# Four graph layers on one core: row ends of the last layer with one product of 128 columns, and GpSimd for their SBUF-only steps

## The chip, the cores and the metric

The kernel runs on one core of one Trainium2 chip. A core has five engines, each with its own queue that is worked off in order: TensorE (PE) multiplies matrices and writes to PSUM, VectorE (DVE) and ScalarE (ACT) compute element by element and read SBUF and PSUM, GpSimd (POOL) computes element by element on SBUF, and SyncE (SP) issues DMAs. The engines wait for each other through semaphores. The time is that of one execution on the device, in microseconds; the metric is the median over several runs.

## The reference

Four layers follow each other over 4096 nodes with 64 features and one weighted adjacency matrix `adj` (4096 x 4096, fp32, all entries at or above zero); each layer's result is added to its input and normalized over the features. Only the last layer, a hyperbolic aggregation, is touched:

```python
c = CURV
deg = jnp.maximum(adj.sum(axis=1, keepdims=True), 1e-08)
w = adj / deg
log_ij = _logmap(x[:, None, :], x[None, :, :], c)
agg = jnp.einsum('ij,ijc->ic', w, log_ij)
transformed = agg @ weight + bias
origin = jnp.zeros_like(transformed)
return _expmap(origin, transformed, c)
...
x = _layernorm(x + _L3_gnn_ref(x, adj, L3_gnn_weight, L3_gnn_bias), axis=-1)
```

`_logmap` of a pair (i, j) is a factor of the pair times a combination of x_i and x_j, so that the sum over j needs, for each row i, a weighted sum of the x_j and a scalar that multiplies x_i. The exponential map at the origin scales each row by tanh of its norm over its norm.

## The kernel before

All of this is the last stage of one program, "layer 3", from line 1423 on. The 4096 nodes are cut into eight groups of 512 (`GB` = 4 blocks of 128). `seq` gives the order of the groups: 4, 5, 6, 7, 0, 1, 2, 3. As the factor of a pair is the same for (i, j) and (j, i), only tiles (i, j) with j at or after i in `seq` are computed, 36 tiles of 512 x 512. Each is done in two halves, so that the loop `while n < NU + 2 ...` runs over 72 units.

In a unit PE multiplies the features (`product`, `opposite`, lines 1493 and 1512), ACT takes five passes over 128x1024 values (square, logarithm, exponentials: lines 1502, 1691, 1692, 1718, 1727), and DVE three products or comparisons of that size (1701, 1704, 1716), a cheap one (1520), and two products of 128x512 with the transposed factors (1540, or 1533 on the diagonal). `gather` then sums on PE: line 1554 the tile's own rows, lines 1562 and 1566 the mirrored ones. The sums go to `tb`, [128, 4096]: its lower half holds a group's own row sum, its upper half the mirrored one (copies on ACT, lines 1573 and 1576). `at_d` and `at_m` are the tiles of `adj`, loaded by SP up to three tiles ahead.

When the last tile of a group's row is summed, `finals(g)` makes the six steps of the group's row end, and they are put on a list, `seam`; every unit takes one step from it. The steps are: nothing; `first`, the products of `tb` with `spread` (the two halves added, 65 columns) and the scalar `al` of each row; `second`, products with `spread_w` (the same with the layer's weight) and of the row's own x with `wh_x`, and from them `v`; `third`, the squared norm of `v` on ACT and its square roots by logarithm and exponential; `fourth`, tanh over norm, applied to `v`, and x added; `fifth`, the layernorm and the output DMA. Six of the eight groups have their row end inside the loop; those of groups 2 and 3, the last in `seq`, are left over when it ends and are done by the last lines, which take a step of one and a step of the other in turn.

The order of the instructions on each engine's queue is set by the tile framework, which places the steps' instructions between those of the units by its own estimate of when they are ready; DVE, ACT and PE work each queue strictly in that order. Tiles come from rotating pools: `r3` holds two buffers of each name (`al`, `v`, `vn`), `ps_p3` two PSUM banks, `post`.

Of the kernel before, what the change touches and what calls it, by code (L numbers as in the profile page):

```python
# [9 lines left out]
F32 = mybir.dt.float32  # L10
# [52 lines left out]
def gnn4_kernel(  # L63
# [22 lines left out]
    P = 128  # L86
# [178 lines left out]
    def layernorm(dst, y, by_ln=False, by_scale=False):  # L265
# [26 lines left out]
        nc.vector.tensor_tensor(dst, y, over_rows(mv[:, :, 0]), ALU.subtract)  # L292
        nc.vector.tensor_tensor(dst, dst, over_rows(r), ALU.mult)
# [1132 lines left out]
    with tc.tile_pool(name="o3", bufs=1) as op, tc.tile_pool(name="cols3", bufs=3) as cols_p, tc.tile_pool(  # L1426
# [9 lines left out]
        spread_w = op.tile([P, F], F32, name="spread_w")  # L1436
# [106 lines left out]
        def gather(t, h, tm):  # L1543
# [30 lines left out]
            if t is not None and h and tiles[t][1] == seq[-1]:  # L1574
                g = tiles[t][0]
                work.append(lambda: nc.scalar.copy(tb[0:F, gcols(g)], bank[0:F, :]))
                seam.extend(finals(g))
            return work

        def factors(ps_p):  # L1580
# [7 lines left out]
            nc.vector.tensor_copy(kappa[:, 1, :], t)  # L1588
# [3 lines left out]
        def weights(ps_p):  # L1592
# [5 lines left out]
            nc.tensor.matmul(ps[:, 0:F], lhsT=t, rhs=wh, start=True, stop=True)  # L1598
            nc.vector.tensor_copy(spread_w, ps[:, 0:F])
# [3 lines left out]


        def finals(g):
# [5 lines left out]
            vn = rp.tile([P, GB, 2], F32, name="vn")  # L1611

            def first(ps_p):
                ps = ps_p.tile([P, GB, F + 1], F32, name="post", tag="post")
                for b in range(GB):
                    nc.tensor.matmul(ps[:, b, :], lhsT=tb[:, cols(g * GB + b)], rhs=spread, start=True, stop=True)
                sq = sm.tile([P, GB, F], F32, name="sq3", tag="t0")
                nc.vector.tensor_tensor(sq, xg, ps[:, :, 0:F], ALU.mult)
                nc.vector.tensor_reduce(al, sq, AX.X, ALU.add)
                nc.vector.scalar_tensor_tensor(al, al, 2.0, ps[:, :, F], ALU.mult, ALU.subtract)  # L1620
                nc.vector.tensor_tensor(al, al, kappa[:, 1, gs], ALU.mult)

            def second(ps_p):
                o = ps_p.tile([P, GB, 2, F], F32, name="post", tag="post")
                for b in range(GB):
                    jb = g * GB + b
                    nc.tensor.matmul(o[:, b, 0, :], lhsT=tb[:, cols(jb)], rhs=spread_w, start=True, stop=True)
                    nc.tensor.matmul(o[:, b, 1, :], lhsT=tr_c[:, jb // 2, :], rhs=wh_x[:, jb % 2, :], start=True, stop=True)
                t = sm.tile([P, GB, F], F32, name="agg", tag="t0")
                for b in range(GB):  # L1630
                    jb = g * GB + b
                    nc.scalar.activation(v[:, b, :], o[:, b, 0, :], AF.Copy, scale=kappa[:, 0, jb : jb + 1])
                nc.vector.tensor_tensor(t, o[:, :, 1, :], over_rows(al), ALU.mult)
                nc.vector.tensor_tensor(t, t, bh.unsqueeze(1).to_broadcast([P, GB, F]), ALU.add)
                nc.vector.tensor_tensor(v, v, t, ALU.add)

            def third(ps_p):

                sq = sm.tile([P, GB, F], F32, name="sqv", tag="t0")
                n = sm.tile([P, GB], F32, name="nv")  # L1640
                for b in range(GB):
                    nc.scalar.activation(sq[:, b, :], v[:, b, :], AF.Square, accum_out=n[:, b : b + 1])
# [5 lines left out]
            def fourth(ps_p):  # L1648
# [7 lines left out]
                nc.vector.tensor_tensor(v, v, over_rows(th), ALU.mult)  # L1656
                nc.vector.tensor_tensor(v, v, xg, ALU.add)

            def fifth(ps_p):
                o_sb = sm.tile([P, GB, F], F32, name="o_sb")  # L1660
                layernorm(o_sb, v, by_ln=True, by_scale=True)
# [17 lines left out]
        while n < NU + 2 or turns or gathers:  # L1679
# [45 lines left out]
            if 0 < n <= NU:  # L1725
                rt = rts[n - 1][:, :, columns(n - 1)]
                nc.scalar.activation(rt, rt, AF.Ln, scale=1.0 / SCALE)  # L1727
            if seam:
                seam.pop(0)(ps_p)
# [55 lines left out]
```

## Time and profile before

| | |
|---|---|
| median of 3 runs | 1419.52 us (1418.89 to 1420.07) |
| profiled execution | 1422.83 us, of which the span is 1421.0 us |
| busy over the span | PE 1322.2 us, DVE 1049.9, ACT 805.8, POOL 99.1 |
| instructions of POOL | 175 |
| granted TensorE clock, mean | 0.972 |
| first steps of the eight row ends (line 1618) begin at | 1091.8, 1169.9, 1236.2, 1294.8, 1339.7, 1374.0, 1395.3, 1397.1 us |
| last products into the sums end at | 1392.4 us |
| last output step ends at | 1417.7 us |

A line of the timeline gives start and duration in us, the engine, the line of the kernel, the operation, the tile written and those read, and their sizes (partitions x elements); in brackets, the idle time of the engine before it and what ended it. A line of the waits gives who waited for whom, the total in us, how often, and the longest. A line of the chain gives start, length and the engine, tile and line that the end of the program hung on at that time. A group's line gives its count, its total and mean time, and the idle time before it. Instructions overlap a little on one engine, so that the time that one takes from its engine is read from its start to the start of the next.

### The profile page before, as it was taken

To read this page: it belongs to the slowest core of one execution; us is meant where nothing else is said; L and a number is where in the kernel's file an instruction comes from. 1 tells how busy PE (TensorE), PEld (TensorE's weight loads), DVE (VectorE), ACT (ScalarE), POOL (GpSimd) and SP (SyncE) were. 2 spreads that over 40 slices of the span, in tenths; PEclk is the share of its full clock that TensorE was granted. 3 is DMA by queue.
4 is the path that set the end of the run, shared out by engine and by line. 5 is a ranking of instruction groups with operands and counts; after the bars stand their busy time and mean duration, and the time that the engine had idled before them with its cause. 6 is when DMAs were issued, how large, how long until landed. Compare 5 with 4: busy or idle time off the path is not lost.

```text
span 1421.0 us, 19096 instructions
## 1 busy us (share of the span) xinstructions
PE 1322.2 (93%) x6830; PEld 616.2 (43%) x6830; DVE 1049.9 (74%) x2016; ACT 805.8 (57%) x1346; POOL 99.1 (7%) x175
## 2 busy tenths in 40 slices
PE   7999999999999998999999999997988898989894
PEld 5655555555344333444443323333333333434433
DVE  7699999998343266878884224357999999998995
ACT  4654444343000116654422675745989999999993
POOL 2111111110132000000110000000000000000000
PEclk9999999999999999999998999998999999999996
DMA  9999999999699999999985555534245344544410
GB/s 321 403 394 415 409 415 415 411 404 393 217 365 389 382 421 378 372 348 335 328 308 178 177 177 175 174 124 178 107 161 207 147 183 152 217 150 170 181 64 11
DMA packets 108191, 382.16 MB, mean 269 GB/s; under 512 B 20276, under 2 KB 20280, under 8 KB 76472
## 3 DMA queue, kind: packets, MB, share of 16 engines
q1 hardware_dynamic: 87096, 296.17, 56.3%
q0 software_dynamic: 12736, 76.29, 13.0%
q10 hardware_dynamic: 8256, 8.39, 1.7%
q8 instruction: 56, 0.92, 0.2%
q14 instruction: 47, 0.39, 0.1%
HBM read 294.05 MB, written 85.20 MB: 267 GB/s over the span
## 4 chain that ended last, share of the span: by engine, by line
PE 64%; ACT 16%; DVE 12%; DMA 5%; issue 2%; ACTq 0%; SPq 0%; DVEq 0%
PE a_ps L1111 8%; PE pass L566 7%; PE tp L657 7%; PE w_ps L566 5%; PE p_ps L1102 5%; PE pass L559 5%; PE cnt_ps L1373 4%; DMA raw<-in_adj_dram 4%; PE h_ps L559 4%; PE acc_ps L1333 4%; ACT w L1691 2%; ACT w L1502 2%; DVE at_m L1540 2%; ACT rt L1692 2%; ACT rt L1727 2%
## 5 line engine op out<-in xcount | busy, mean ns | idle before, releaser
L664 ACT COPY at<-tp 128x512 f32<-128x512 f32 x248 | 127.8, 598 | 118.2 <-issue 95.0
L1378 ACT ACTIVATE wt<-cnt_ps 128x512 uint16<-128x512 f32 x208 | 115.5, 595 | 73.1 <-PE cnt_ps L1373 68.2
L688 DVE TENSOR_REDUCE dpart<-raw 128x4 f32<-128x2048 f32 x64 | 145.5, 2274 | 4.0 <-DMA raw<-in_adj_dram 3.9
L1554 PE MATMUL sums_ps<-at_d,some 128*64 128x512 f32 x288 | 146.2, 628 | 2.0 <-DVE at_d L1533 1.8
L690 DVE TENSOR_REDUCE lows<-raw 128x1 f32<-128x2048 f32 x64 | 145.5, 2273 | 0.0
L657 PE MATMUL tp<-ident,raw 128*128 128x128 f32 x1024 | 130.8, 281 | 7.9 <-DMA raw<-in_adj_dram 6.6
L657 PEld LDWEIGHTS tp<-ident,raw 128*128 128x128 f32 x1024 | 114.5, 143 | 45.4 <-issue 35.1
L1111 PE MATMUL a_ps<-at,nat_a 128*64 128x512 f32 x512 | 123.4, 610 | 0.0
L1566 PE MATMUL sums_ps<-at_m,some 128*64 128x512 f32 x224 | 110.5, 616 | 0.0
L1493 PE MATMUL v_ps<-rv,tr_a 64*128 64x512 f32 (+1 forms) x288 | 81.9, 647 | 21.8 <-DVE rt L1716 21.6
L566 PE MATMUL pass<-at,cheb_n 128*128 128x512 f32 x224 | 99.2, 601 | 2.4 <-DVE cheb_n L588 1.9
L566 PE MATMUL w_ps<-at,cheb_n 128*128 128x512 f32 x208 | 93.5, 593 | 0.0
L1716 DVE SCALAR_TENSOR_TENSOR rt<-v_ps,rt 128x1024 f32<-128x1024 f32 x72 | 83.2, 1156 | 4.3 <-ACT rt L1692 4.0
L1373 PE MATMUL cnt_ps<-m,follow 128*64 128x512 fp8e4 x480 | 81.7, 391 | 4.6 <-ACT wt L1378 2.0
L1701 DVE SCALAR_TENSOR_TENSOR f<-rt,w 128x1024 f32<-128x1024 f32 x72 | 82.8, 1156 | 2.8 <-ACT rt L1727 2.7
L1704 DVE TENSOR_TENSOR at_d<-at_d,f 128x1024 f32<-128x1024 f32 x72 | 83.0, 1153 | 0.1
L1380 DVE TENSOR_SCALAR wt<-cnt_ps 128x512 uint16<-128x512 f32 x48 | 33.2, 692 | 63.2 <-PE cnt_ps L1373 60.1
L1540 DVE TENSOR_TENSOR at_m<-post,at_m 128x512 f32<-128x512 f32 x112 | 74.6, 679 | 4.6 <-PE post L1538 4.5
L1727 ACT ACTIVATE rt<-rt 128x1024 f32<-128x1024 f32 x72 | 72.4, 1006 | 9.7 <-DVE rt L1716 9.4
L1538 PE MATMUL post<-ident,f 128*128 128x128 f32 x448 | 69.3, 284 | 7.2 <-DVE at_m L1540 6.2
L1691 ACT ACTIVATE w<-w 128x1024 f32<-128x1024 f32 x72 | 72.0, 1001 | 5.0 <-DVE w L1520 5.0
L1718 ACT ACTIVATE w<-w 128x1024 f32<-128x1024 f32 x72 | 72.3, 1006 | 0.7
(392 smaller groups left out, 2250.8 us busy)
## 6 DMA issues: line engine op xcount, KB each, us to landing
at<-adj_t SPq DMA_DIRECT2D x119, 1024.0 KB, 7.6
raw<-in_adj_dram SPq DMA_DIRECT2D x64, 1024.0 KB, 13.1
adj_t<-at POOLq DMA_DIRECT2D x62, 1024.0 KB, 8.0
at_d<-adj_t SPq DMA_DIRECT2D x36, 1024.0 KB, 4.6
at_m<-adj_t SPq DMA_DIRECT2D x28, 1024.0 KB, 6.7
m<-mask_t SPq DMA_DIRECT2D x120, 128.0 KB, 2.8
m<-mask_t SPq DMA_DIRECT2D x60, 256.0 KB, 4.2
mask_t<-mask ACTq DMA_DIRECT2D x28, 256.0 KB, 7.6
```

The source lines that it names most:

```text
L559: in_order(nc.tensor.matmul(ps[q * F : (q + 1) * F, :], lhsT=cheb_n[:, jb, k, :], rhs=rhs, start=first, stop=last, skip_group_check=True,))
L566: in_order(nc.tensor.matmul(ps, lhsT=cheb_n[:, jb, k : k + 2, :], rhs=rhs, start=first, stop=last))
L657: in_order(nc.tensor.transpose(tp[:, cols(b)], raw[:, b, cols(k)], ident))
L664: nc.scalar.copy(at[:, k, :], tp)
L688: in_order(nc.vector.tensor_reduce(dpart[:, g, c, :], raw, AX.X, ALU.add))
L690: in_order(nc.vector.tensor_reduce(lows[:, n : n + 1], raw.rearrange("p b j -> p (b j)"), AX.X, ALU.min))
L1111: in_order(nc.tensor.matmul(ps[q * F : (q + 1) * F, :], lhsT=nat_a[:, c * CB + k, 0:F], rhs=of[q if signed else 0][:, k, :], start=(c == 0 ...
L1373: in_order(nc.tensor.matmul(cnt[a][r * HP : (r + 1) * HP, :], lhsT=follow, rhs=chunks[c][odd][2 * a + r][:, k, :], start=(h == 2 * NB - 1) ...
L1378: in_order(nc.scalar.activation(wt[odd][a], cnt[a], AF.Relu, scale=-128.0))
L1540: work.append(lambda to=to, tp=tp: nc.vector.tensor_tensor(to, tp, to, ALU.mult))
L1554: in_order(nc.tensor.matmul(bank[0:F, :], lhsT=nat_c[:, j * CB + k, :], rhs=own[t][:, k, :], start=(i == j and k == 0), stop=(j == seq[-1] ...
L1566: in_order(nc.tensor.matmul(bank[F:P, :], lhsT=nat_c[:, above * GB + k, :], rhs=mirrored[tm][:, k, :], start=(k == 0 and above == seq[0]), ...
```

## The change

The change has five parts, all in the row ends of layer 3 and the step that prepares them.

- `spread` and `spread_w` stand side by side in one tile, `two_w`, and `first` makes one product of 128 columns of each block of `tb` instead of one of 65 and, later, one of 64. The extra column that `first` used is replaced by a tile `z`: x less its last feature, with -0.5 in the last column, made by GpSimd in `less_last`; kappa's second part holds twice its value.
- For the last two groups the products of x with `wh_x` are made before, by two steps (`ahead_of_last`) that are put on the list six units before the end; ACT copies them to SBUF (`turned_x`).
- For these two groups `v` is scaled by DVE in `first`, and the rest stays on DVE and ACT.
- For the other six groups GpSimd adds the bias, adds the two parts of `v`, squares `v`, and later scales `v` and adds x; DVE sums the squares, where ACT squared and summed before; and the layernorm ends with two products on GpSimd in place of four scaled outputs on ACT.
- The last copy of `tb`'s lower half goes from ACT to DVE.

In the changed kernel as built, the queue of SP keeps its order. The two steps made ahead take two places of the list, so that the steps of group 1 come two units later; its statistics and layernorm are then done after the loop.

```diff
-    def layernorm(dst, y, by_ln=False, by_scale=False):
+    def layernorm(dst, y, by_ln=False, by_scale=False, last=None):
+        last = last or nc.vector
...
-        nc.vector.tensor_tensor(dst, y, over_rows(mv[:, :, 0]), ALU.subtract)
-        nc.vector.tensor_tensor(dst, dst, over_rows(r), ALU.mult)
+        last.tensor_tensor(dst, y, over_rows(mv[:, :, 0]), ALU.subtract)
+        last.tensor_tensor(dst, dst, over_rows(r), ALU.mult)
...
-        spread_w = op.tile([P, F], F32, name="spread_w")
+        two_w = op.tile([P, 2 * F], F32, name="two_w")
+        spread_w = two_w[:, F : 2 * F]
...
-                work.append(lambda: nc.scalar.copy(tb[0:F, gcols(g)], bank[0:F, :]))
+                copy = nc.vector.tensor_copy if g == seq[-1] else nc.scalar.copy
+                work.append(lambda: copy(tb[0:F, gcols(g)], bank[0:F, :]))
...
-            nc.vector.tensor_copy(kappa[:, 1, :], t)
+            nc.vector.tensor_scalar_mul(kappa[:, 1, :], t, 2.0)
...
+            nc.vector.tensor_copy(two_w[:, 0:F], pair)
...
+        turned_x, zs = {}, {}
+
+        def less_last(g):
+            z, xg = rp.tile([P, GB, F], F32, name="z"), nat_a[:, gblocks(g), 0:F]
+            nc.gpsimd.tensor_tensor(z[:, :, 0 : F - 1], xg[:, :, 0 : F - 1], over_rows(xg[:, :, F - 1], F - 1), ALU.subtract)
+            nc.gpsimd.memset(z[:, :, F - 1], -0.5)
+            return z
+
+        def weighed_x(ps_p, g):
+            o = ps_p.tile([P, GB, F], F32, name="post", tag="post")
+            for b in range(GB):
+                jb = g * GB + b
+                nc.tensor.matmul(o[:, b, :], lhsT=tr_c[:, jb // 2, :], rhs=wh_x[:, jb % 2, :], start=True, stop=True)
+            return o
+
+        def ahead_of_last(g):
+            def step(ps_p):
+                turned_x[g] = rp.tile([P, GB, F], F32, name="xw")
+                nc.scalar.copy(turned_x[g], weighed_x(ps_p, g))
+                zs[g] = less_last(g)
+
+            return step
...
+            late = g in seq[-2:]
+            own_engine = nc.vector if late else nc.gpsimd
+
+            z = zs[g] if late else less_last(g)
...
-                ps = ps_p.tile([P, GB, F + 1], F32, name="post", tag="post")
+                ps = ps_p.tile([P, GB, 2 * F], F32, name="post", tag="post")
                 for b in range(GB):
-                    nc.tensor.matmul(ps[:, b, :], lhsT=tb[:, cols(g * GB + b)], rhs=spread, start=True, stop=True)
+                    nc.tensor.matmul(ps[:, b, :], lhsT=tb[:, cols(g * GB + b)], rhs=two_w, start=True, stop=True)
                 sq = sm.tile([P, GB, F], F32, name="sq3", tag="t0")
-                nc.vector.tensor_tensor(sq, xg, ps[:, :, 0:F], ALU.mult)
+                nc.vector.tensor_tensor(sq, z, ps[:, :, 0:F], ALU.mult)
                 nc.vector.tensor_reduce(al, sq, AX.X, ALU.add)
-                nc.vector.scalar_tensor_tensor(al, al, 2.0, ps[:, :, F], ALU.mult, ALU.subtract)
                 nc.vector.tensor_tensor(al, al, kappa[:, 1, gs], ALU.mult)
-
-            def second(ps_p):
-                o = ps_p.tile([P, GB, 2, F], F32, name="post", tag="post")
+                if late:
+                    nc.vector.tensor_tensor(v, ps[:, :, F : 2 * F], over_rows(kappa[:, 0, gs]), ALU.mult)
+                    return
                 for b in range(GB):
                     jb = g * GB + b
-                    nc.tensor.matmul(o[:, b, 0, :], lhsT=tb[:, cols(jb)], rhs=spread_w, start=True, stop=True)
-                    nc.tensor.matmul(o[:, b, 1, :], lhsT=tr_c[:, jb // 2, :], rhs=wh_x[:, jb % 2, :], start=True, stop=True)
+                    nc.scalar.activation(v[:, b, :], ps[:, b, F : 2 * F], AF.Copy, scale=kappa[:, 0, jb : jb + 1])
+
+            def second(ps_p):
                 t = sm.tile([P, GB, F], F32, name="agg", tag="t0")
-                for b in range(GB):
-                    jb = g * GB + b
-                    nc.scalar.activation(v[:, b, :], o[:, b, 0, :], AF.Copy, scale=kappa[:, 0, jb : jb + 1])
-                nc.vector.tensor_tensor(t, o[:, :, 1, :], over_rows(al), ALU.mult)
-                nc.vector.tensor_tensor(t, t, bh.unsqueeze(1).to_broadcast([P, GB, F]), ALU.add)
-                nc.vector.tensor_tensor(v, v, t, ALU.add)
+                nc.vector.tensor_tensor(t, turned_x[g] if late else weighed_x(ps_p, g), over_rows(al), ALU.mult)
+                own_engine.tensor_tensor(t, t, bh.unsqueeze(1).to_broadcast([P, GB, F]), ALU.add)
+                own_engine.tensor_tensor(v, v, t, ALU.add)
+                if not late:
+                    nc.gpsimd.tensor_tensor(z, v, v, ALU.mult)
 
             def third(ps_p):
...
+                if late:
+                    for b in range(GB):
+                        nc.scalar.activation(sq[:, b, :], v[:, b, :], AF.Square, accum_out=n[:, b : b + 1])
+                else:
+                    nc.vector.tensor_reduce(n, z, AX.X, ALU.add)
...
-                nc.vector.tensor_tensor(v, v, over_rows(th), ALU.mult)
-                nc.vector.tensor_tensor(v, v, xg, ALU.add)
+                own_engine.tensor_tensor(v, v, over_rows(th), ALU.mult)
+                own_engine.tensor_tensor(v, v, xg, ALU.add)
...
-                layernorm(o_sb, v, by_ln=True, by_scale=True)
+                layernorm(o_sb, v, by_ln=True, by_scale=late, last=own_engine)
...
+            if n == NU - 6:
+                seam += [ahead_of_last(g) for g in seq[-2:]]
```

More of the change, by code (lines that the diff above doesn't have):

```diff
@@ L1611, in finals @@
             vn = rp.tile([P, GB, 2], F32, name="vn")
+            n = rp.tile([P, GB], F32, name="nv")
+            late = g in seq[-2:]
+            own_engine = nc.vector if late else nc.gpsimd
+            z = zs[g] if late else less_last(g)
             def first(ps_p):
-                ps = ps_p.tile([P, GB, F + 1], F32, name="post", tag="post")
+                ps = ps_p.tile([P, GB, 2 * F], F32, name="post", tag="post")
                 for b in range(GB):
-                    nc.tensor.matmul(ps[:, b, :], lhsT=tb[:, cols(g * GB + b)], rhs=spread, start=True, stop=True)
+                    nc.tensor.matmul(ps[:, b, :], lhsT=tb[:, cols(g * GB + b)], rhs=two_w, start=True, stop=True)
@@ L1637, in third @@
+                if not late:
+                    nc.gpsimd.tensor_tensor(z, v, v, ALU.mult)
             def third(ps_p):
                 sq = sm.tile([P, GB, F], F32, name="sqv", tag="t0")
-                n = sm.tile([P, GB], F32, name="nv")
-                for b in range(GB):
-                    nc.scalar.activation(sq[:, b, :], v[:, b, :], AF.Square, accum_out=n[:, b : b + 1])
+                if late:
[3 more added lines that the diff above has]
+                    nc.vector.tensor_reduce(n, z, AX.X, ALU.add)
```

## The prediction

> **What bounds the kernel now.** The change touches layer 3 alone, so after the page I read the busy time of two stretches: the loop over the tiles of layer 3 (to the last product into sums) and what follows it.
>
> ```profile
> 985.00:1392.00 407.00, 364.67 (x1717) 153.68 (x1717) 386.26 (x652) 377.44 (x536) 0.62 (x2) 0.96 0.41 158
> 1392.00:1421.00 29.00, 10.34 (x51) 9.56 (x48) 12.20 (x70) 11.54 (x52) 0.00 (x0) 0.55 0.06 14
> ```
>
> Columns: stretch, length, busy PE, PEld, DVE, ACT, POOL, granted clock, DMA share, GB/s. In the loop DVE is busy 95% and ACT 93% of the time, while GpSimd does nothing and the DMA engines are 41% busy. After it no engine is full: there the time is a chain of handovers at half clock. Then DVE's waits in the loop:
>
> ```profile
> DVE w L1520 <- ACT w L1502: 5.4, 6, 1.8
> DVE at_m L1540 <- PE post L1538: 4.5, 4, 2.0
> DVE rt L1716 <- ACT rt L1692: 4.0, 6, 2.5
> DVE f L1701 <- ACT rt L1727: 2.7, 5, 0.6
> ```
>
> DVE waits some 19 us in 407. So what is taken from DVE comes out of the loop, and what DVE stands idle goes into it. Third, the timeline of DVE where a group's row end lies inside the loop:
>
> ```profile
> 1100.36 0.42 DVE L1634 TENSOR_TENSOR agg<-agg,bh 128x256 f32<-128x256 f32 x1
> 1102.12 0.42 DVE L1635 TENSOR_TENSOR v<-v,agg 128x256 f32<-128x256 f32 x1
> 1102.45 0.69 DVE L1520 TENSOR_SCALAR w<-w 128x1024 f32<-128x1024 f32 x1
> 1112.31 0.42 DVE L1656 TENSOR_TENSOR v<-v,th 128x256 f32<-128x256 f32 x1
> 1112.64 1.22 DVE L1716 SCALAR_TENSOR_TENSOR rt<-v_ps,rt 128x1024 f32<-128x1024 f32 x1
> 1113.78 0.41 DVE L1657 TENSOR_TENSOR v<-v,nat_a 128x256 f32<-128x256 f32 x1
> ```
>
> Each holds DVE for 0.33 us from start to next start (1112.31 to 1112.64). Fourth, the chain that ended last, in order of time, and the timeline of the last output step:
>
> ```profile
> 1394.17 2.86 PE post L1616 x16
> 1398.34 0.66 PE post L1627 x2
> ...
> 1404.97 0.44 PE post L1628 x2
> 1410.23 0.42 DVE v L1656
> 1416.41 1.32 ACT o_sb L290 x4
> ```
>
> The second products of the last two groups fill PE from 1398.34 to 1405.41, 7.1 us in which everything else waits. The last products into sums end at 1392.43 (1391.84 and 0.59), the last output step at 1417.73: 25.3 us of tail. Fifth, GpSimd, by form and in the timeline, and what DVE did beside it:
>
> ```profile
> L622 POOL TENSOR_TENSOR nat_a<-nat_a,cheb_n 128x256 f32<-128x256 f32 x8 | 5.8, 731 | 17.3 <-DVE cheb_n L588 17.3
> 534.36 1.19 POOL L233 MEMSET with_ones<- 128x4 f32 x1
> 533.93 1.57 DVE L500 TENSOR_SCALAR first_pos<-at 128x2048 fp32r<-128x2048 f32 x1
> 535.68 1.21 DVE L500 TENSOR_SCALAR pos<-at 128x2048 fp32r<-128x2048 f32 x1
> ```
>
> GpSimd's product of 128x256 takes 0.73 us against DVE's 0.42. And the two engines held each other up once: the memset of 128x4 took 1.19 (median of its eight: 0.115) and ended with L500, which took 1.57 (median 1.23).
>
> **The change, part by part.** All sums are against the profiled execution: 1422.83 us, 1421.0 of it span; that is 3.3 above the median of the runs, 1419.52, and I carry the difference found over to the median. 0.2%, about what a measurement can tell from no change, is 2.8 us.
>
> *Work leaving DVE, ACT and PE in the six groups.* Per group DVE loses four products (4 x 0.33) and two steps of 128x4 (2 x 0.07 from start to start), and gains the reduce for the norm (0.33): -1.13, six times -6.8. ACT loses four squares (0.97, 1103.20 to 1104.16) and four scaled outputs (1.32, 1124.29 to 1125.61): -2.3 per group. PE loses 8 records of 0.11. DVE is the fuller engine and every unit passes through it, so I count its 6.8 and nothing more.
>
> *Three GpSimd steps in second, and DVE's reduce behind them.* The bias, the sum and the square are a chain of three: 3 x 0.73 and three handovers of some 0.06 (between DVE and ACT one takes 0.04 to 0.05), 2.37 us. DVE keeps its order: as built, agg is followed by one product of 128x1024 (f or at_d) and then by the reduce that waits for the square. That holds for groups 4, 5, 6 and 0; group 7 has three operations in between, group 1 two halves. What counts is whether GpSimd may run beside that product, which reads two SBUF tiles, as GpSimd does. If not, the chain begins when the product ends, and DVE idles 2.37 in four groups, 0.8 in group 7 and 1.6 in group 1: 11.8. If it may, 1.13 of each chain is covered: 4 x 1.28, 0 and 1.1, 6.2. No row shows two readers side by side. The nearest two disagree: L500 and the memset blocked each other, while the product L1701 beside a memset, which only writes, was untouched (1.22 at 1007.04). I take the first, since the new GpSimd steps read SBUF as well as write it, and keep the second for the range.
>
> The Trainium skill (SBUF — State Buffer, Who interferes with whom) says that a DVE instruction with two SBUF inputs contends with a GpSimd instruction that reads SBUF, and that the later one is blocked for the whole instruction; it speaks against this change. By that rule the sum is the one I take; by the memset row alone it would be the rival with free ports.
>
> *Two GpSimd steps in fourth, and the statistics behind them.* 2 x 0.79 between th and DVE's first statistic. In between DVE has one operation of 0.60 in groups 4 and 5, four in group 6, two in 7 and 0. Blocked ports: 0.8, 0.8, 0, 1.6, 1.6, together 4.8; free ports: 0.6, 0.6 and nothing, 1.2. Queued behind the waiting instruction are the next at_m and rt, and so PE's next product and ACT's next exponential.
>
> *Three more GpSimd steps per group* (x less its last column, and the two of the layernorm) have nobody waiting soon, but run into DVE's stream. One that starts with an at_m product (0.60) ends 0.13 into the two-input product after it: 18 x 0.13 = 2.3, between 0 and 18 x 0.73 = 13. I take 2.3, because every second operation of DVE reads PSUM. The output DMA of these groups is issued later by the layernorm's 1.5 us, and SP's loads behind it with it; tiles are loaded ahead, SP's order is the same, and a load lands in 4.6 to 6.7 us of a tile's 10 to 11: nothing, at worst 1.5 in a few groups.
>
> *Into the loop's end:* two copies of 128x256 on ACT (0.37 each, L1219's row) and eight products of 64 columns, beside full DVE: nothing. Their two places in the list of row-end steps push group 1's steps two units back, so its statistics now stand on DVE between the last products and the copy of tb.
>
> *The tail.* Counted from the end of the last products. Group 1's GpSimd pair ends at about 0.35; eight statistics and ve take 1.2 (1391.27 to 1392.44), then DVE's copy of tb, 0.68 as L1396's of that size: 2.2, where ACT's two copies were done at 1.7. First four products: 1.2 as before (1394.17 to 1395.34), since a load of 128 columns sets the pace, not 65 or 128 moving ones: 3.4. Group 3 on DVE: square with x and v 2 x 0.33, reduce 0.47, al 0.2, three products 1.4: 6.1. The other four products at half clock end near 5.2, hidden. Group 2 the same on DVE: 8.9. Four squares 1.0: 9.9. From nv to th, 2.45 (1409.28 to 1411.71): 12.35. The two products 0.95: 13.3. Statistics 1.2, then root to scale 1.9: 16.4. Outputs 1.3: 17.7. That is 7.6 less than 25.3, nearly all of it the 7.1 of the second products. Bounds: 6 to 8.
>
> *Start of the layer:* the first two groups' x less last column, one wider table and a factor 2 in kappa: GpSimd idles there for tens of us; nothing.
>
> Sum: -6.8 + 11.8 + 4.8 + 2.3 - 7.6 = +4.5. Forecast: 1419.5 + 4.5 = **1424.0 us**.
>
> **The rivals.**
> 1. *Free ports (faster).* GpSimd's reads do not hold up DVE's two-input products. For: the untouched L1701. Against: the memset of 1.19. Then -6.8 + 6.2 + 1.2 + 0 - 7.6 = -7.0: 1412.5. It decides as soon as DVE's added stalls stay under 14.4, the sum of relief and tail.
> 2. *GpSimd dearer than L622's row.* The new steps spread one factor over 64 columns, which L622 does not. At 1.0 us each, 0.27 more, five in chains in five groups and three in the sixth give 28 x 0.27 = 7.6: 1431.6. Against: L622's eight lie within 0.722 to 0.742.
> 3. *The change does less than it says:* DVE's stalls only replace some of the 19 us that it waits anyhow. With a quarter of these swallowed, -4.7: about 1419. For: those waits lie in the same units; against: they are waits for ACT and PE, which come late by the same stall.
>
> **How the numbers follow.** Blocked ports 0.66, with its own range 1420.5 to 1428 (GpSimd at 0.65 or 0.80 us moves it by 3, the tail by 1.5); the third rival is its lower part, 0.12 of the 0.66. Free ports 0.26. Dearer GpSimd 0.08. The range for 8 in 10, 1411.5 to 1430, takes in the free ports and leaves out most of the dearer case. Slower by over 2.8: 0.54 of the first and most of the third, 0.60. Within: 0.16. Faster: the free ports but for a bit, 0.24.
>
> **What would show it.** Right: DVE's waits list the norm's reduce and the first statistic behind GpSimd, 2.4 and 0.8 to 1.6 each, some 16 us in all; the GpSimd products in layer 3 show spans over 0.73, or DVE's two-input ones over 1.22; tail 17 to 18.5 us, with no second product of 64 columns in it. The forecast is wrong if these waits sum to under 9 us, if two-input products keep 1.22 beside GpSimd, or if the tail is not shorter by 6.

## The result and the profile after

The changed kernel takes 1430.33 us (median, 1428.51 to 1434.3) against 1418.89 us for the kernel before on the same chip: a ratio of 1.0079, 95% interval 1.0061 to 1.0097. It is slower by 11 us, in the direction of the forecast (1424.0 us) and 0.3 us above the upper end of its range (1430.0). Its profiled execution took 1431.03 us, 1429.1 of it span, against 1422.83 and 1421.0 before.

The busy time by stretch of the changed kernel, with the columns of the first view of the prediction (stretch, length, busy PE, PEld, DVE, ACT, POOL, clock, DMA share, GB/s), from the first product of layer 3 to the last product into the sums, and from there to the end:

```profile
978.99:1407.70 428.71, 373.93 (x1704) 154.91 (x1703) 391.00 (x644) 371.71 (x476) 47.69 (x54) 0.93 0.42 157
1407.70:1429.10 21.40, 2.05 (x16) 1.86 (x16) 14.08 (x75) 8.12 (x39) 1.43 (x3) 0.68 0.08 18
```

The kernel before, cut at the same two events:

```profile
977.49:1392.43 414.94, 368.19 (x1736) 155.45 (x1735) 393.82 (x681) 382.81 (x542) 0.62 (x2) 0.96 0.42 163
1392.43:1421.00 28.57, 9.91 (x49) 9.56 (x48) 11.81 (x67) 11.54 (x52) 0.00 (x0) 0.55 0.06 14
```

So the loop is 13.8 us longer and what follows 7.2 shorter. In the loop DVE is busy 2.8 us less, and idle, length less busy time, 16.6 us more (21.1 to 37.7). ACT has not become the bound: its busy time fell by 11 us. DVE's waits in the loop of the changed kernel say whom it stood for:

```profile
DVE at_m L1542 <- PE post L1540: 10.8, 11, 2.8
DVE nv L1675 <- POOL z L1666: 10.3, 6, 2.1
DVE w L1522 <- ACT w L1504: 5.7, 7, 1.5
...
DVE ln_st L271 <- POOL v L1690: 2.5, 3, 1.3
```

10.3 us behind the chain of three GpSimd steps and 2.5 behind the pair in `fourth`, neither of which was there before; the wait for PE's transposes rose from 4.5 to 10.8. The timeline at the row end of group 4 shows how one of these waits comes about and where it goes:

```profile
1099.03 0.42 DVE L1662 TENSOR_TENSOR agg<-post,al 128x256 f32<-128x256 f32 x1
1099.49 1.23 DVE L1734 SCALAR_TENSOR_TENSOR f<-rt,w 128x1024 f32<-128x1024 f32 x1
1099.53 1.77 POOL L1663 TENSOR_TENSOR agg<-agg,bh 128x256 f32<-128x256 f32 x1 [90.99 <-ACT rt L1760]
1101.38 0.73 POOL L1664 TENSOR_TENSOR v<-v,agg 128x256 f32<-128x256 f32 x1
1102.19 0.61 POOL L1666 TENSOR_TENSOR z<-v 128x256 f32<-128x256 f32 x1
1102.83 0.42 DVE L1675 TENSOR_REDUCE nv<-z 128x4 f32<-128x256 f32 x1 [2.12 <-POOL z L1666]
...
1104.30 1.10 DVE L1522 TENSOR_SCALAR w<-w 128x1024 f32<-128x1024 f32 x1
1105.43 1.06 ACT L1724 ACTIVATE w<-w 128x1024 f32<-128x1024 f32 x1 [2.09 <-DVE w L1522]
...
1107.79 1.23 PE L1495 MATMUL v_ps<-rv,tr_a 64*128 64x512 f32 x2 [4.26 <-DVE rt L1749]
```

GpSimd's first product starts 0.04 us after DVE's product of two SBUF tiles and takes 1.77 us: it ends 0.58 us after that product has ended (1100.72), which is about its own length. The other two follow in 1.4 us. DVE's next instruction is the reduce; it stands 2.12 us, and what is queued behind it comes late with it: ACT waits 2.09 us for `w`, PE 4.26 us for `rt`. Groups 5, 6 and 0 have the same 2.12 us, groups 7 and 1 have 0.5 and 1.3; in a second profile of the changed kernel these waits again sum to 10.3 us.

In the tail the second products are gone: sixteen products of 128 columns are all that PE does.

```profile
1407.11 0.59 PE L1568 MATMUL sums_ps<-at_m,some 128*64 128x512 f32 x1
...
1409.74 2.05 PE L1648 MATMUL post<-two_w,tb 128*128 128x128 f32 x16 [2.04 <-DVE tb L1579]
...
1424.46 1.43 ACT L291 ACTIVATE o_sb<-v,ln_s,ln_r 128x64 f32<-128x64 f32 x4 [1.37 <-DVE ln_s L289]
```

From the end of the last product into the sums, 1407.70, to the end of the last output step, 1425.89, it is 18.2 us, where it was 25.3.

### The profile page after: what moved, and what is told of

Its sections match the earlier page's. It is cut to its first block, busy times and chain, and to the rows that moved or that the text cites. A ratio compares the mean times of both kernels' runs of the same rounds, so it can differ in the third digit from the quotient of the medians.

```text
span 1429.1 us, 18944 instructions
## 1 busy us (share of the span) xinstructions
PE 1320.5 (92%) x6766; PEld 609.0 (43%) x6766; DVE 1050.6 (74%) x1988; ACT 791.2 (55%) x1267; POOL 148.5 (10%) x233
## 5 line engine op out<-in xcount | busy, mean ns | idle before, releaser
L1556 PE MATMUL sums_ps<-at_d,some 128*64 128x512 f32 x288 | 152.0, 650 | 2.0 <-DVE at_d L1535 1.4
L1495 PE MATMUL v_ps<-rv,tr_a 64*128 64x512 f32 (+1 forms) x288 | 84.8, 668 | 32.9 <-DVE rt L1749 32.4
L1542 DVE TENSOR_TENSOR at_m<-post,at_m 128x512 f32<-128x512 f32 x112 | 74.5, 684 | 11.1 <-PE post L1540 10.8
L1724 ACT ACTIVATE w<-w 128x1024 f32<-128x1024 f32 x72 | 71.8, 1000 | 15.0 <-DVE w L1522 14.9
L1556 PEld LDWEIGHTS sums_ps<-at_d,some 128*64 128x64 f32 x288 | 35.4, 145 | 90.7 <-issue 72.9
```

The lines of the kernel that those rows point to most:

```text
L1495: in_order(nc.tensor.matmul(vs[n][:, k, cs], lhsT=tr_c[half, jb // 2, :], rhs=rights[i][0][half, cs], start=True, stop=True))
L1556: in_order(nc.tensor.matmul(bank[0:F, :], lhsT=nat_c[:, j * CB + k, :], rhs=own[t][:, k, :], start=(i == j and k == 0), stop=(j == seq[-1] ...
```

## The experiments

All ratios are to the kernel before on the same chip (its median 1419.4 to 1420.1 us in these comparisons). "Loop" is the stretch from the first product of layer 3 to the last product into the sums, "tail" from there to the last output step, "idle" DVE's idle time in the loop, all from the profiled execution. Runs 1 to 4 were made on one chip and runs 5 to 12 on another; loops and tails of different runs are set beside each other all the same, and a difference of 1 us between two of them means little.

| | loop | idle | tail | time | ratio, 95% interval |
|---|---|---|---|---|---|
| before | 414.9 | 21.1 | 25.3 | 1418.9 to 1420.1 | 1 |
| changed | 428.7 | 37.7 | 18.2 | 1430.33 | 1.0079 (1.0061 to 1.0097) |
| 1: DVE keeps the steps | 414.3 | 21.4 | 18.0 | 1414.15 | 0.9966 (0.9949 to 0.9983) |
| 2: GpSimd's part alone | 425.8 | 35.9 | 24.7 | 1438.26 | 1.014 (1.0116 to 1.0164) |
| 3: two empty steps | 422.3 | 30.0 | 19.0 | 1423.50 | 1.0039 (1.0021 to 1.0057) |
| 4: longer chain | 427.6 | 34.2 | 19.6 | 1428.18 | 1.0065 (1.0044 to 1.0087) |
| 5: layernorm pair alone | 415.2 | 22.1 | 18.0 | 1414.65 | 0.997 (0.9956 to 0.9984) |
| 6: norm chain alone | 428.9 | 35.8 | 18.0 | 1428.92 | 1.0072 (1.0053 to 1.0092) |
| 7: th pair alone | 411.2 | 22.3 | 18.3 | 1412.21 | 0.9954 (0.9937 to 0.9971) |
| 8: spare products | 423.4 | 20.2 | 18.0 | 1427.07 | 1.0055 (1.0039 to 1.0071) |
| 9: all but the chain | 410.7 | 21.5 | 19.1 | 1410.78 | 0.9924 (0.9897 to 0.9952) |
| 10: chain without the square | 416.1 | 21.4 | 18.1 | 1418.48 | 0.9983 (0.9964 to 1.0002) |
| 11: chain, reduce later | 416.4 | 24.4 | 22.3 | 1419.82 | 0.9991 (0.9974 to 1.0007) |
| 12: change, reduce later | 412.1 | 20.8 | 19.8 | 1413.67 | 0.9953 (0.9933 to 0.9972) |

**1 and 2: the two halves of the change.** The first takes GpSimd's part back and keeps the rest:

```diff
-            own_engine = nc.vector if late else nc.gpsimd
+            own_engine = nc.vector
...
-                if not late:
-                    nc.gpsimd.tensor_tensor(z, v, v, ALU.mult)
...
-                if late:
-                    for b in range(GB):
-                        nc.scalar.activation(sq[:, b, :], v[:, b, :], AF.Square, accum_out=n[:, b : b + 1])
-                else:
-                    nc.vector.tensor_reduce(n, z, AX.X, ALU.add)
+                for b in range(GB):
+                    nc.scalar.activation(sq[:, b, :], v[:, b, :], AF.Square, accum_out=n[:, b : b + 1])
...
-                layernorm(o_sb, v, by_ln=True, by_scale=late, last=own_engine)
+                layernorm(o_sb, v, by_ln=True, by_scale=True)
```

> The changed kernel with the row end's GpSimd part taken back: in the six groups inside the loop DVE again adds bias and sum, scales by th, adds x and, with ACT, ends the layernorm, and ACT squares for the norm. Kept: the product of 128 columns, x less its last column on GpSimd, the last two groups weighed ahead, the copy of tb on DVE. Theory 1 (the loss is DVE standing behind GpSimd's steps): the waits of the norm's reduce and of the first statistic behind GpSimd are gone, the loop of layer 3 (first product to last product into sums) goes from 428.7 us back to 414 to 417, the tail stays at 18.2, the time is 1411 to 1415, some 7 below the kernel before. Rival (the loss comes from the reordering: two row-end steps put ahead, group 1 two units later, the wider product in the loop): the loop stays above 424 and the time at 1422 to 1430.

The second keeps GpSimd's part and does the last two groups as before (`finals_before` is the `finals` of the kernel before):

```diff
-                copy = nc.vector.tensor_copy if g == seq[-1] else nc.scalar.copy
+                copy = nc.scalar.copy
...
+            if g in seq[-2:]:
+                return finals_before(g)
...
-            if n == NU - 6:
-                seam += [ahead_of_last(g) for g in seq[-2:]]
```

> GpSimd's part alone: the six groups inside the loop as in the changed kernel, the last two as in the kernel before (two products, nothing weighed ahead, the copy of tb on ACT, group 1's steps not shifted). Theory 1: the loop of layer 3 is 425 to 430 us, the tail 25 to 26, the time 1431 to 1438, slower than the changed kernel by about the tail's 7 us or a little less. Rival (reordering): the loop falls to 414 to 419 and the time is 1418 to 1424.

Without GpSimd's part the loop is back at 414.3 us with the tail at 18.0: the reordering costs nothing that shows, and this half of the change makes the kernel faster. GpSimd's part alone has a loop of 425.8 and is slower than the changed kernel by the tail. The loss lies in the six groups' GpSimd steps, as theory 1 says. The two steps made ahead and the shift of group 1 are no cause.

**5, 6 and 7: which of GpSimd's three parts.** Each adds one part to run 1.

```diff
 5    layernorm(o_sb, v, by_ln=True, by_scale=late, last=nc.vector if late else nc.gpsimd)
 6    as the changed kernel, but
      nc.vector.tensor_tensor(v, v, over_rows(th), ALU.mult)
      nc.vector.tensor_tensor(v, v, xg, ALU.add)
      layernorm(o_sb, v, by_ln=True, by_scale=True)
 7    pair_engine = nc.vector if late else nc.gpsimd
      pair_engine.tensor_tensor(v, v, over_rows(th), ALU.mult)
      pair_engine.tensor_tensor(v, v, xg, ALU.add)
```

> As the run in which DVE keeps the row-end steps (1414.15 us, loop of layer 3 414.3), but GpSimd does the layernorm's last two products in the six groups, which nothing but the output's DMA waits for. By the prediction's terms against that run: DVE loses 2 steps of 0.07 us, ACT its four scaled outputs, and 12 GpSimd products run into DVE's stream at 0.13 each, 1.6: -0.8 + 1.6 = +0.8, time 1414 to 1416. If GpSimd's products cost nothing where nobody waits (free ports): 1413 to 1414, or less where ACT's 8 us of relief count. If every one holds DVE for its whole 0.6 us: +7, 1421.

> The changed kernel with only the first of GpSimd's parts: bias, sum and square in the second step, and DVE's reduce of the norm behind them; the products with th and x and the layernorm's end are DVE's and ACT's again. By the prediction's terms, against the run in which DVE keeps all (1414.15, loop 414.3): DVE loses 2 x 0.33 and gains 0.33 in six groups, -2.0; the waits for the chain as measured in the changed kernel, +10.3; products that hold up DVE, +1 to 2: +9 to 10, time 1423 to 1425, loop 423 to 425. If these waits also bring PE below full clock (theory 2: gaps of PE of 2 to 4.3 us are followed by 3.4 to 6.8 us at half clock in the changed kernel), +13 to 16: time 1427 to 1431, half clock in the loop 40 us or more against 20. If the chain is not the main cause: below 1419.

> As the run in which DVE keeps the row-end steps, but GpSimd does the two products of the fourth step (v with th, plus x) in the six groups, with DVE's first statistic behind them. By the prediction's terms: DVE loses 2 x 0.33 in six groups, -4.0; waits of the first statistic 4.1 as measured in the changed kernel, of which 2.5 in the loop; 12 products at 0.13 to 0.3, 1.6 to 3.6: +1 to +3, time 1415 to 1418. These waits are 1.5 us at most; if PE's gaps behind them stay under 2 us, the clock does not fall and nothing is added. If it falls all the same: 1419 to 1423.

Against run 1 the layernorm's pair adds 0.9 us to the loop, the norm chain 14.6, and the pair with th takes 3.0 off; together 12.5, of the changed kernel's 14.4. The chain alone gives the whole loss. The first line of DVE's waits in the run with the chain alone:

```profile
DVE nv L1675 <- POOL z L1666: 12.7, 6, 2.1
```

DVE's idle time is 14.5 us above that of run 1, and this wait is 12.7 of it: here all six groups wait 2.1 us, where groups 7 and 1 of the changed kernel wait 0.5 and 1.3. The time, 1428.92, lies in the range that was given for waits that also bring half clock (51 us of it in the loop), and above the 1423 to 1425 for the waits alone; but as the waits came out longer, some 2 of the 14.6 us are left for anything besides them. The pair with th was forecast to lose and gains. In its run, the timeline where DVE meets it at group 4:

```profile
1109.59 0.69 DVE L1522 TENSOR_SCALAR w<-w 128x1024 f32<-128x1024 f32 x1
1109.82 0.93 POOL L1685 TENSOR_TENSOR v<-v,th 128x256 f32<-128x256 f32 x1 [17.77 <-ACT rt L1721]
1110.19 1.22 DVE L1745 SCALAR_TENSOR_TENSOR rt<-v_ps,rt 128x1024 f32<-128x1024 f32 x1
1110.83 0.73 POOL L1686 TENSOR_TENSOR v<-v,nat_a 128x256 f32<-128x256 f32 x1
...
1111.59 0.35 DVE L271 BATCH_NORM_STATS2 ln_st<-v 128x6 f32<-128x64 f32 x2 [0.17 <-POOL v L1686]
```

Here DVE has `w` and a product that reads PSUM between th and the statistic, so the pair runs beside them and DVE waits 0.17 us; over the loop these waits are 0.8 us, and the idle time is that of run 1 to 1 us.

**3, 4: more time for the chain, and a longer chain.**

```diff
 3
+            if g in seq[:4]:
+                return [nothing, first, second, nothing, third, fourth, nothing, fifth]
             return [nothing, first, second, third, fourth, fifth]
 4
-                    nc.gpsimd.tensor_tensor(z, v, v, ALU.mult)
+                    for _ in range(3):
+                        nc.gpsimd.tensor_tensor(z, v, v, ALU.mult)
```

> The changed kernel with an empty place in the list of row-end steps before the norm's reduce and before the layernorm, in the first four groups (4, 5, 6, 7), so that GpSimd has one unit of the loop more before DVE needs its result. No work is added or taken away; groups 0 and 1 come as much later as the list makes them. Theory 1 with blocked ports (DVE stands for the handover, not for lack of capacity): the waits of the norm's reduce (2.4 us each in groups 4, 5, 6) and of the first statistic (0.8 to 1.6) vanish in these four groups, and with them their echo in PE and ACT; what GpSimd's products wait for the port stays. Loop shorter by 8 to 11 us, time 1419 to 1423. Rival (the loss is GpSimd's products holding up DVE's and being held up themselves, the port's throughput, whoever waits): the time stays within 3 us of the changed kernel.

> The changed kernel with GpSimd's square of the row end done three times over (the same result each time), so that the chain in front of DVE's reduce of the norm is longer by two products, 2 x 0.67 = 1.34 us, in six groups. If a wait of DVE costs its own length and no more, the loop is longer by 6 x 1.34 = 8.0 us, or 6.7 where group 7's is covered: time 1437 to 1438.5. If every wait comes back as an echo in ACT and PE (theory 2: in the changed kernel 12.5 us of such waits in the loop came with 6 us more of DVE waiting for PE), it is longer by 10 to 13: time 1440 to 1444. If other work covers the chain (rival), under 4: below 1435.

With the empty steps the reduce's wait is left in groups 0 and 1 alone (4.2 us), and the loop is 6.4 us shorter, 1.6 less than expected: DVE's idle time fell by 7.7, but its busy time rose by 1.3, since GpSimd's products now met more of its own. The longer chain was a miss for every theory: with two products more the waits fell, from 10.3 to 7.4 us, and the loop did not grow. The timeline at group 4 of that run says why:

```profile
1096.59 0.42 DVE L1662 TENSOR_TENSOR agg<-post,al 128x256 f32<-128x256 f32 x1
1097.05 2.89 DVE L1735 SCALAR_TENSOR_TENSOR f<-rt,w 128x1024 f32<-128x1024 f32 x2
...
1099.87 1.75 DVE L1738 TENSOR_TENSOR at_d<-at_d,f 128x1024 f32<-128x1024 f32 x1
1100.61 3.21 POOL L1667 TENSOR_TENSOR z<-v 128x256 f32<-128x256 f32 x3
1101.54 1.22 DVE L1750 SCALAR_TENSOR_TENSOR rt<-v_ps,rt 128x1024 f32<-128x1024 f32 x1
...
1103.86 0.42 DVE L1676 TENSOR_REDUCE nv<-z 128x4 f32<-128x256 f32 x1 [0.50 <-POOL z L1667]
```

The framework orders by its own estimate of when a result is ready. Told of a longer chain, it set the reduce six places behind the product with al instead of two, and DVE waited 0.50 us instead of 2.12. This points to the place of the reduce in DVE's queue, and not to the length of the chain; but the order of much else changed as well, so runs 10 to 12 change the place in other ways.

**10: the chain without its reduce.** GpSimd adds bias and sum, ACT squares and sums as before.

```diff
-                own_engine.tensor_tensor(t, t, bh.unsqueeze(1).to_broadcast([P, GB, F]), ALU.add)
-                own_engine.tensor_tensor(v, v, t, ALU.add)
+                sum_engine.tensor_tensor(t, t, bh.unsqueeze(1).to_broadcast([P, GB, F]), ALU.add)
+                sum_engine.tensor_tensor(v, v, t, ALU.add)
```

(`sum_engine` is GpSimd in the six groups; all else is run 1.)

> GpSimd adds bias and sum in the second step of the six groups, as in the changed kernel, but ACT squares for the norm as before, so that DVE has no reduce of 128x256 to make behind GpSimd; as built, the first operation of DVE that needs the result stands six operations behind the product with al instead of two. All else as in the run in which DVE keeps the steps (1414.15). If the place of the waiting reduce in DVE's order makes the loss, and not GpSimd's work: DVE loses 4 x 0.33 / 2 = 0.66 us in six groups, -4.0, 12 products hold it up by 0.13 to 0.18 each, +2: time 1411 to 1414, loop 410 to 414. If the first two GpSimd steps cost by themselves (ports, or ACT waiting for v instead of DVE): 1418 to 1426.

Neither side has it whole, and the time, 1418.48, lies in the range of the second. The wait of the reduce is gone, and the idle time is 21.4 as in run 1 (in group 7 alone DVE waits 1.5 us for the norm, by way of ACT). But the loop is 1.8 us longer than run 1's, though DVE is relieved of 4.0 us of products: its busy time rose by 1.8. The timeline shows what it is busy with:

```profile
1096.95 2.90 DVE L1730 SCALAR_TENSOR_TENSOR f<-rt,w 128x1024 f32<-128x1024 f32 x2
1097.07 1.69 POOL L1664 TENSOR_TENSOR agg<-agg,bh 128x256 f32<-128x256 f32 x1 [3.26 <-DVE agg L1663]
1098.84 1.59 POOL L1665 TENSOR_TENSOR v<-v,agg 128x256 f32<-128x256 f32 x1
1099.77 1.74 DVE L1733 TENSOR_TENSOR at_d<-at_d,f 128x1024 f32<-128x1024 f32 x1
```

Three products of two SBUF tiles stand in a row here. The two `f` take 2.90 us where two take 2.36 undisturbed (1.14 from start to start, and 1.22), and `at_d` 1.74 for 1.22; GpSimd's products take 1.69 and 1.59. The engines take turns here, and each turn costs DVE some 0.5 us. They do not always: in group 7 of the same run GpSimd's product stands through three such products of DVE, which are not held up.

```profile
1300.94 2.35 DVE L1730 SCALAR_TENSOR_TENSOR f<-rt,w 128x1024 f32<-128x1024 f32 x2
1301.17 3.84 POOL L1664 TENSOR_TENSOR agg<-agg,bh 128x256 f32<-128x256 f32 x1 [2.10 <-DVE agg L1663]
1303.21 1.22 DVE L1733 TENSOR_TENSOR at_d<-at_d,f 128x1024 f32<-128x1024 f32 x1
```

What decides between the two was not found out. In run 7, whose two GpSimd products are of the same size, they ran beside `w`, at_m and rt and averaged 0.67 and 0.78 us, and DVE's busy time fell by 3.9, though `w` was held up in three groups (0.79 to 1.06 us for 0.69).

**11 and 12: the reduce one unit later.** The same instructions as run 6 and as the changed kernel, with one empty place in the list before `third` in the six groups; the steps behind `third` come later with it.

```diff
+            if not late:
+                return [nothing, first, second, nothing, third, fourth, fifth]
             return [nothing, first, second, third, fourth, fifth]
```

> The run with the chain alone (1428.92 us, loop of layer 3 428.9) with one empty place more in the list of row-end steps between the second and the third step of the six groups: every instruction is the same, but in groups 4, 5, 6 and 7 DVE's reduce of the norm now stands 8 or 9 operations behind the product with al instead of 2; in groups 0 and 1 the list leaves it 1 or 2 behind. If its place makes the loss: the waits of groups 4, 5, 6 and 7 go (8.2 of 12.7), 4.2 stay in groups 0 and 1; loop 418 to 421, time 1417 to 1421. If GpSimd's chain costs wherever the reduce stands: loop 425 or more, time above 1425.

> The changed kernel (1430.33 us, loop 428.7) with the same empty place. If the place makes the loss: nv waits of groups 4, 5, 6 and 7 gone, 4.2 left; with what the pair with th gained alone (3.0 in the loop) and the layernorm's pair (0.9 lost), loop 415 to 420, time 1415 to 1421: slower than the run with all but the chain (410.7; 1410.8), because products that hold DVE up eat what DVE is relieved of. If the place does not matter: 425 or more, time above 1425.

The loop of run 6 falls by 12.5 us, that of the changed kernel by 16.6, with every product of GpSimd still there. The changed kernel with one empty place takes 1413.67 us and is faster than the kernel before. Both loops are shorter than expected, since the waits in groups 0 and 1, which were expected to stay, left the loop too: in group 0 the reduce waits 0.5 us in run 11 and not at all in run 12, and in group 1 it now stands in the tail and waits 2.3 us there (the tails are 4.3 and 1.6 us longer). The timeline of run 12 at group 4:

```profile
1096.97 2.89 DVE L1736 SCALAR_TENSOR_TENSOR f<-rt,w 128x1024 f32<-128x1024 f32 x2
1097.01 1.77 POOL L1663 TENSOR_TENSOR agg<-agg,bh 128x256 f32<-128x256 f32 x1 [90.23 <-ACT rt L1762]
...
1099.79 1.75 DVE L1739 TENSOR_TENSOR at_d<-at_d,f 128x1024 f32<-128x1024 f32 x1
1100.53 1.47 POOL L1666 TENSOR_TENSOR z<-v 128x256 f32<-128x256 f32 x1
...
1106.26 0.41 DVE L1675 TENSOR_REDUCE nv<-z 128x4 f32<-128x256 f32 x1
```

The square is done at 1102.0 and the reduce comes at 1106.26 without a wait. The engines hold each other up more than in the changed kernel (`f` 2.89, `at_d` 1.75), and it does not matter: DVE's idle time is 16.9 us less.

**8: the price of a GpSimd product that nobody waits for.** Run 1 plus 12 products a group on GpSimd that nothing reads.

```diff
+                if not late:
+                    spare = rp.tile([P, GB, F], F32, name="spare")
+                    for _ in range(12):
+                        nc.gpsimd.tensor_tensor(spare, z, z, ALU.mult)
```

> The port's price by itself: as the run in which DVE keeps the row-end steps, plus 12 GpSimd products of 128x256 per group in the second step of six groups, 72 in all, which read x less its last column and write a tile that nothing reads. DVE's and PE's own work is unchanged. Free ports: 0, time 1413 to 1416, each product 0.6 us long. The prediction's 0.13 each: +9.4, time 1422 to 1425. Two engines taking turns at a whole instruction's length, where about one product in three holds DVE for 0.3 to 0.6 us: +7 to +14, GpSimd's products showing spans of 0.6 to 1.8 and DVE's two-input ones 1.5 to 1.8 instead of 1.22. If every product holds DVE for all its length: +44.

24 of the 72 ran before layer 3's loop, where x less its last column is ready early (0.61 us each); 48 ran in it. By form, in the loop (count, total and mean ns, idle before):

```profile
L1668 POOL TENSOR_TENSOR spare<-z 128x256 f32<-128x256 f32 x48 | 47.2, 983 | 3.8
```

The mean is 0.98 us where an undisturbed one takes 0.61; DVE's busy time rose by 10.3 us (392.9 to 403.2), its idle time fell by 1.2, and the loop grew by 9.1: 0.19 us a product. Free ports are excluded, and so is a price of the whole product. The prediction's 0.13 was of the right order and too small by a third. The time grew by 12.9 us, 4 more than the loop, and lies above the 1422 to 1425 of that price; the first product of layer 3 came 3.2 us later than in run 1, and whether the 24 products ahead of it have to do with that is not shown.

**9: what the parts point to.** GpSimd keeps x less its last column, the pair with th and the layernorm's pair; the chain and the norm go back to DVE and ACT (run 7 with the layernorm line of run 5).

> The changed kernel with the chain of the second step and the norm given back to DVE and ACT, and all else of GpSimd's part kept: x less its last column, v with th plus x, the layernorm's last two products. From the runs of each alone: the pair with th gave -1.9 us against 1414.15, the layernorm's pair +0.5: 1412.7, in 1411 to 1415, faster than both kernels. If GpSimd's steps, nearer together, hold each other up, the first statistics wait longer and it is 1415 to 1418.

It has a loop of 410.7 us and takes 1410.78, a little below the range given for it and the fastest of all, 0.76% below the kernel before (0.48 to 1.03%).

**The two kernels once more.**

> The kernel before, unchanged, profiled a second time: what differs between two executions of one program. The first profile had 1422.83 us, 3.4 above the median of the runs of before made so far (1419.4), a granted clock of 0.972 and 34 us at half clock in the loop of layer 3. If the scatter between executions comes with the half-clock stretches (over 23 runs of before the time rises 0.23 us per us at half clock, correlation 0.76), an execution at a clock of 0.976 or above has 1416 to 1420 us, with the difference in the stages where the clock differs. If it does not, time and clock part.

> The changed kernel, unchanged, profiled a second time. The first profile had 1431.03 us, clock 0.967, 61 us at half clock in the loop of layer 3. Theory: the long waits of the norm's reduce return at the same places and lengths (2.1 us in groups 4, 5, 6 and 0, 10 us in all), half clock in the loop is 48 us or more again, since PE's gaps behind them stay at 3.7 to 4.3 us; time 1427 to 1433. If the half clock was chance, it is below 40 us.

The kernel before took 1416.99 us in its second profile, the changed one 1430.70. The loop of the kernel before is 414.8 us against 414.9, and its tail 24.2 against 25.3; that of the changed kernel is 429.4 against 428.7, and 18.2 both times. So layer 3 repeats within 1.2 us, while its first product came at 977.5 and 972.9 in one and the same program: the scatter between executions lies mostly ahead of layer 3.

## Why the prediction was right and wrong

- *Relief of DVE, -6.8.* Nearly right. DVE's busy time fell by 2.8 us in spite of 4.1 by which GpSimd held single instructions up (the sum over eleven of them of what they took above the same instruction undisturbed): 6.9. But some 1.2 of it are group 1's statistics, which left the loop for the tail, so that GpSimd's part took nearer 5.7 off DVE.
- *The chain in `second`, 11.8.* The mechanism was right and is shown: run 6 alone has the loss, runs 11 and 12 take it away by moving the reduce, and runs 3, 4 and 10 agree. The choice between the two bounds was right as well; the row at 1099.53 fits a GpSimd that is blocked until DVE's product ends. The waits measured 10.3 us, a little less because the second and third product take 0.73 and 0.61.
- *The pair in `fourth`, 4.8.* Too dear. 2.5 us in the loop of the changed kernel, and 0.8 with the pair alone, where DVE mostly has `w` and rt in between. The 0.8 that it counts for groups 4 and 5 do not follow from its own numbers either: 2 x 0.79 less 0.60 is 0.98. Alone the pair gains: its step in the sum would have been -4.0 + 0.8 and some holding up, not -4.0 + 4.8 + 1.6.
- *What the waits bring with them, no term at all.* This is the step of the sum that failed. The prediction names PE's next product and ACT's next exponential as queued behind the waiting instruction, and counts nothing for them. The two kinds of wait are 12.8 us, DVE's idle time rose by 16.6: the other 3.8 had no term. ACT and PE do come late, as in the rows at 1105.43 and 1107.79. But how the 3.8 come about one by one is not shown. DVE's wait for the transposes, 10.8 us against 4.5 before, is no measure of it, for run 1, which has no wait behind GpSimd and no more idle time than the kernel before, has most of it too:

```profile
DVE at_m L1542 <- PE post L1540: 8.6, 8, 3.2
```

  The third rival, that the new waits take the place of old ones, was wrong by its sign. That the idle time came out at 11.8 + 4.8 is luck: 3.8 too much in these two terms, and 3.8 left out.
- *Three more GpSimd steps, 2.3.* The term for being held up was mis-sized: 4.1 us, of which 3.0 beside the three steps that it covers and 1.0 beside the chain and the pair, for which it has nothing. The step counted the products of two SBUF tiles alone; five of the eleven held instructions are `w` (1.10 us for 0.69, as at 1104.30), which reads one tile, five more are the small `ln_ve` and `nv`, and only one is a product of two SBUF tiles.
- *The tail, -7.6.* Right, -7.1 (and -6.0 against the second profile of before); run 1 shows it alone.
- *Layer 3 as a whole:* forecast +4.5, measured +6.7 between the first profiles and +8.6 between the second ones.
- *The second step that failed* is "I carry the difference found over to the median". The comparison gives 0.79% of 1419, 11.2 us (8.7 to 13.8), 2.6 to 4.5 more than layer 3 holds. With layer 3's own difference the time would have been 1426 to 1428, inside the range. The rest lies ahead of layer 3, where the order of PE, ACT, DVE and SP is the same in both kernels, and where two executions of one program differ by 4.6 us. In the fourteen profiles of the changed kernel and of runs 1 to 12 the first product of layer 3 comes at 975.7 to 980.2 us, in the two of the kernel before at 972.9 and 977.5. Whether the difference there is scatter or an effect of the change stays open.
- *Its signs.* The waits sum to 12.8 us in the loop, over the 9 that it asked for, and the tail is as it said. Its sign against itself, that products of two SBUF tiles keep 1.22 us beside GpSimd, is there by the letter in the changed kernel (1.23 at 1099.49, and no whole one longer), since there GpSimd came second and was the one held up. In runs 4, 10 and 12 GpSimd came between two of them, and the later one takes some 1.75. The sign could not tell the two cases apart.
- *The range* ended at 1430.0, below a case with all of it together: the waits, what they bring with them, and the scatter. Free ports, the rival on the other side, are excluded by run 8; dearer GpSimd products too, since undisturbed ones take 0.61 us, or 0.73 behind another GpSimd step, and not 1.0. (In the free ports' sum 2.37 less 1.13 is 1.24 and not 1.28, which makes 0.2 us in all.)

## What to carry to other kernels

When work moves to another engine, look first at what stands next in the queue of the engine that needs the result, and how many places behind the moment at which the chain can start: here two places or ten, in four of six groups, decided between 1430 and 1414 us, with the same instructions. An order made from estimated times seems here not to count that two engines hold each other up, so that a result comes later than the order supposes (here a product took 1.77 us for 0.61); an empty step in the list is a cheap way to give it that time. Then choose for the second engine the steps that can run beside instructions that read PSUM: two products of the same size cost DVE some 0.5 us each beside products of two SBUF tiles in run 10, and little beside others in run 7.

## What the runs showed of the hardware

Being held up is not for products of two tiles alone: `w`, a comparison that reads and writes one SBUF tile of 128x1024 in 0.69 us, took 1.10 beside GpSimd's product (1104.30, above). The Trainium skill (SBUF — State Buffer, Who interferes with whom) names this case too: an operation of this kind can run in a mode that uses both port pairs, and then contends with GpSimd. The trace agrees; the prediction had used only the page's sentence on two SBUF inputs. A product that reads PSUM and one SBUF tile kept 1.22 us beside GpSimd (1110.19 in run 7).

Behind the long waits TensorE also runs below its full clock. The same stretch of group 4 in the changed kernel, 2 us at a time (the granted clock is the third number from the end):

```profile
1102.00:1104.00 2.00, 1.12 (x8) 0.68 (x7) 1.17 (x2) 1.34 (x2) 1.39 (x3) 1.00 0.66 279
1104.00:1106.00 2.00, 0.00 (x0) 0.00 (x0) 2.00 (x4) 0.57 (x1) 1.44 (x2) 0.69 0.00 0
1106.00:1108.00 2.00, 0.21 (x2) 0.21 (x4) 2.00 (x3) 2.00 (x4) 0.00 (x0) 0.50 0.00 0
...
1112.00:1114.00 2.00, 2.00 (x10) 0.60 (x8) 2.00 (x4) 1.47 (x3) 0.00 (x0) 1.00 0.28 53
```

PE stands from 1103.53 to 1107.79, the clock is halved from 1104.8 to 1111.6, and the four products into `v_ps` take 2.08 us where they take 1.13 at full clock. In the whole loop half clock was granted for 61 us of the changed kernel against 34 before, and for 24 with the reduce later; in the second profile of the changed kernel the same stretch is at half clock again (51 us in the loop). What this costs the loop could not be told apart from the waits that go with it. Over 23 runs of the kernel before the time rises by 0.23 us for each us at half clock (correlation 0.76), which does not say which brings which; and the two profiles of the kernel before have 34 and 24 us at half clock in loops of 414.9 and 414.8 us, so these 10 us, most of them at the start of layer 3, cost the loop nothing that shows.
